# A graph layer's opening reordered: searches, flags, splits and the first block's chunk sums placed behind the first product

## The chip, the cores and the metric

The kernel runs on one core of a Trainium2 chip, in one launch. The metric is the device time of the whole launch in microseconds, smaller is better. The five engines with a queue of their own are TensorE (PE in the profile, with PEld for its weight loads), VectorE (DVE), ScalarE (ACT), GpSimd (POOL) and SyncE (SP, which here only issues DMAs). Each executes its queue in the order in which the program emits it.

## The reference

```python
def ref(x, src, dst, edge_attr, W1, b1, W2, b2):     # x 6250x64, 206250 edges sorted by dst
    h = max(layernorm(x), 0)
    msg = h[src] + edge_attr                          # edge_attr 206250x64
    agg = segment_sum(msg, dst, 6250)
    return x + relu(agg @ W1 + b1) @ W2 + b2          # W1 64x128, W2 128x64
```

All is float32. The edges come sorted by destination node; each node has some 33 of them.

## The kernel before, in words

The sum over `h[src]` is done as a product with counts: for each target node and each of the 6250 source nodes, how many edges go from one to the other. A source node's number is split into a low digit (128 rows) and a high one (49 values). For a *tile* of up to 127 edges of three neighbouring target nodes (a *triple*), TensorE multiplies a one-hot of the low digit by a one-hot of the high digit weighted by the node within the triple (`count`, line 957, out `pc`, 12 tiles at a time); ScalarE copies the counts out of PSUM into a ring in SBUF (line 966). For a *block* of 84 tiles (252 target nodes) TensorE then multiplies the table `h`, split into an upper and a lower half so that the product is exact enough (`h2`, written by `split_upper` and `split_lower`), by the counts: `products` (line 976), 49 matmuls into `pv`, in four parts of 12 or 13. VectorE makes the codes (`encode`, 927 and 933) and the one-hots (`rows_of_tiles`, 944, `hotb`).

The sum over `edge_attr` goes another way: *chunks* of 42 nodes' edges are loaded in order (`load_chunk`, 462, `feat`), VectorE makes a one-hot of each edge's distance to its chunk's first node (`chunk_hot`, 475, `hotf`), and TensorE sums (`chunk_sum`, 486, into `bank`, 48 matmuls). `take_sums` (494) copies a block's sums out, and `chunk_place` (516) adds them to the block's product. `open_gathers` lets GpSimd copy one element of those sums, so that its later gathers stand behind it. The distances come from a gather (`fetch_dst`) at indices that `chunk_columns` and `chunk_index` make; `chunk_nodes` subtracts (426, 427), `chunk_turn` transposes (434, 435) into `rel`.

The last 20 groups of edges are done by gathering rows of a table of `h` in DRAM (`fetch_h`, `hrows`), which `norm_h` writes in three thirds after scaling (595, 596).

To know where a group of tiles begins in the sorted list, the kernel fetches rows of 256 destinations (`fetch_row`), searches in them on ScalarE (`seek`, 354, with a read-back of the accumulator), and writes the starts (`place`, 359 and 361). With them it fetches the edges' packed words in pairs (`fetch_pair`), unpacks them on VectorE in four pieces (`unpack`: fields, offsets, inside, digits), transposes them (`turn_keys` 763, `turn_values` 770) and copies the keys and powers to `kq` and `kv` (783, 791). Fourteen triples with more than 127 edges get a second tile each: `second_ends`, `second_flags`, `second_ranks`, `second_picks`, `second_words`, `second_found` find them, alternating between VectorE and TensorE (`pnext`, `prk`, `pxn`), and `second_fetch` and one more `unpack` bring them in.

The order of all this is written out by hand. The main loop runs over 318 *steps* of six tiles, 14 to a block; block 0's counts are steps 0 to 13, and block `b`'s product runs in steps 1, 3, 5 and 7 of block `b+1` (block 0's in steps 15, 17, 19, 21). The table `before` says what is emitted ahead of a step's count, `SPLITS`, `CLEARS` and `SECOND` add to it, `turn_later` and `at_step` put work behind a step. GpSimd's gathers stand in a list `queue`, drawn from by a planned clock (`pool_until`), except where a function issues them at once.

```python
    for n in range(NSTEP):
        b, s = block_of(n)
        for f in tops.get(n, []) + before.get(n, []):
            f()
        if n % 2:
            count(n)
        if n % (HT // ST) == 0:
            rows_of_tiles(n // (HT // ST) + 1)
        if n % (EB // ST) == AHEAD and n // (EB // ST) * EB + EB < TILES:
            encode(n // (EB // ST) + 1)
        if b and 1 <= s < FRESH:
            products(b - 1, PART[s], PART[s + 1])
        ...
        for f in later.pop(n, []) + turns.pop(n, []):
            f()
```

Of the kernel before, what the change touches and what calls it, by code (L numbers as in the profile page):

```python
# [22 lines left out]
P = 128  # L23
# [41 lines left out]
NX = 14  # L65
# [14 lines left out]
SPLITS = (9, 10, 11)  # L80
CLEARS = (61, 47, 33, 19, 17)
SECOND = (10, 11, 12, 13, 14, 15, 16)
# [3 lines left out]
FIRST_CHUNKS = ((13, 13), (14, 14), (14, 14))  # L86
FIRST_HOT_AT = (11, 12, 14)
# [65 lines left out]
def gnn_kernel(ctx: ExitStack, tc: tile.TileContext, x, src_t, dst_t, dst_g, edge, w1, b1, w2, b2, out):  # L153
# [242 lines left out]
    def chunk_columns(t0, t1, tag="po", bufs=1):  # L396

        px = ps.tile([P, NT + 1], F32, tag=tag, name="pcols", bufs=bufs)
        quarters = known.pop(("q", t0))
        rows = [(t, quarters[:, (t - t0) * RC:(t - t0 + 1) * RC, :]) for t in range(t0, t1)]  # L400
        if t0 == 0:
            rows.append((NT, row_n))
        for t, of in rows:
            nc.tensor.matmul(px[:, t:t + 1], of.rearrange("o c q -> o (c q)"), ones[0:1, 0:1], start=True, stop=True)
        known["t", t0] = px
# [59 lines left out]
    def load(u):  # L465
        for k in range(GB):
            load_chunk(u, k)
# [247 lines left out]
    def unpack(i0, n, p, base, checked):  # L715
        words = words_of.pop(i0)[:p, :n]
        code = late.tile([P, 3, 2, 2, P], I16, name="code")
# [156 lines left out]
    def second_fetch():  # L874
        queue.insert(0, (WORDS_US / 2, lambda: fetch_words(2 * PC, 1, NX, [flags.pop("i")[:, :]])))
# [263 lines left out]
    fetch_pair(2)  # L1139
# [5 lines left out]
    chunk_columns(0, 2, "pc", 2)  # L1145
    seek(7, 4)
# [3 lines left out]
    def first_loads():  # L1150
# [5 lines left out]
        1: [lambda: norm_h(0), lambda: chunk_index(0, 2), lambda: fetch_dst(0), lambda: fetch_dst(1)],  # L1156
        2: [lambda: norm_h(1), lambda: norm_h(2), lambda: [fetch_h(g) for g in range(GA, GA + ROWS)]],
        3: [first_loads, lambda: seek(11, 2)],
        4: [lambda: load(1)],
        5: [lambda: seek(13, IC - 13), lambda: load(2)],  # L1160
        6: [lambda: place(7, IC - 7)],
        8: [lambda: chunk_nodes(0)],
        9: [lambda: chunk_turn(0)],
        16: [find_groups],
# [43 lines left out]
    for i in range(1, IC):  # L1208
        c0, c1 = columns(i)[0][2], columns(i)[-1][2] + columns(i)[-1][1] - columns(i)[-1][0]
        n = min((n for n in range(deadline(c0) + 1 - TURN[-1][0]) if n % STEPS in (TURNS if i > 2 else (2,)) and c1 - R <= encoded(n)),  # L1210
# [8 lines left out]
    n = 23  # L1219
    assert n + TURN[-1][0] <= deadline(SX)  # L1220
    unpack_later(n - 4, lambda: unpack(2 * PC, 1, NX, second_b, NX))
    turn_later(n, 2 * PC, NX, [(0, NX, SX)])
    for t in range(1, NT):
        n = 78 + 14 * t
        before.setdefault(n, []).append(lambda t=t: t > 1 and queue.insert(0, (GATHER_US, lambda: fetch_dst(t))))
        n = 33 if t == 1 else 87 + 14 * t
# [23 lines left out]
    for b in range(NW):  # L1250
# [6 lines left out]
        if b < NW - 1:  # L1257
            at_step(n + STEPS + TAKE, take_sums, b)
            at_step(n + STEPS + TAKE, open_gathers, b)
            for u in of_block[b]:  # L1260
                at_step(n + STEPS + PLACE, chunk_place, u)
# [237 lines left out]
```

## Time and profile before

| | |
|---|---|
| Median of three runs | 400.97 us (399.53 to 402.68) |
| Profiled execution | 401.95 us, its span 399.9 us |
| TensorE busy | 334.5 us (84%) |
| VectorE busy | 321.0 us (80%) |
| ScalarE busy | 322.8 us (81%) |
| GpSimd busy | 240.4 us (60%) |
| DMA | 77.73 MB, mean 194 GB/s |
| Mean granted clock of TensorE | 0.987 |

The span is the time from the first to the last instruction; what lies around it is the launch. A row of the order in time reads: start and length in us, engine, line, operation, what it writes and from what, how many instructions were merged, and in brackets how long the engine stood idle ahead of it and what ended that. A queue's own entries have a q behind the engine's name. A row of the windows has the busy time and the count of instructions of PE, PEld, DVE, ACT and POOL, then the granted clock, the busy share of the DMA engines and GB/s.

### The profile page before, as it was taken

How to read it: one execution, taken by the hardware profiler on the slowest of the kernel's cores; microseconds unless marked ns; L12 is line 12 of the kernel's file. 1: busy time of each engine (PE TensorE's matmuls, PEld its weight loads, DVE VectorE, ACT ScalarE, POOL GpSimd, SP SyncE). 2: the span in 40 equal slices, each digit the busy share in tenths (PEclk: the TensorE clock that was granted, in tenths of full speed). 3: DMA queues.
4: the chain of work that ended last, by engine and by line, in shares of the span. 5: the costliest groups of instructions: out<-in, count | busy, mean ns of one | idle time of the engine just before them, and what ended most of it. 6: DMA issues, size and time to landing. Idle time of an engine off the chain costs nothing.

```text
span 399.9 us, 17302 instructions
## 1 busy us (share of the span) xinstructions
PE 334.5 (84%) x7299; PEld 307.1 (77%) x7300; DVE 321.0 (80%) x833; ACT 322.8 (81%) x376; POOL 240.4 (60%) x254
## 2 busy tenths in 40 slices
PE   2025259689988899989999999999999999999993
PEld 1024149688987798877889988999998999999882
DVE  5969694799899778996789896998799889978620
ACT  5446876669998777898899999999899889988740
POOL 8888687746775665744745677738776576501200
PEclk9999999989998999999999999999999999999998
DMA  7946957556958576684975786786679678755600
GB/s 161 285 126 204 319 140 215 156 147 201 227 180 253 131 221 166 178 264 127 275 219 154 237 247 185 221 259 201 203 236 261 178 200 262 200 161 183 174 11 10
DMA packets 97345, 77.73 MB, mean 194 GB/s; under 512 B 14388, under 2 KB 90284, under 8 KB 97262
## 3 DMA queue, kind: packets, MB, share of 16 engines
q1 hardware_dynamic: 88480, 66.72, 54.9%
q0 software_dynamic: 6544, 9.06, 9.8%
q8 instruction: 59, 0.97, 1.0%
q10 hardware_dynamic: 2238, 0.79, 0.8%
q14 instruction: 24, 0.20, 0.1%
HBM read 72.29 MB, written 4.26 MB: 191 GB/s over the span
## 4 chain that ended last, share of the span: by engine, by line
PE 52%; DVE 15%; ACT 10%; issue 3%; DVEq 0%; ACTq 0%
PE pv L976 26%; PE pc L957 8%; ACT ring L966 7%; PE bank L486 6%; DVE hotb L944 5%; PE po L1062 3%; PE pv L516 2%; PE ph L1054 2%; PE bank L547 2%; DVE hotf L475 2%; PE pk L763 1%; ACT over L892 1%; ACT after L1056 1%; DVE sums L1011 1%; DVE at L927 1%
## 5 line engine op out<-in xcount | busy, mean ns | idle before, releaser
L966 ACT ACTIVATE ring<-pc 128x1764 fp32r<-128x1764 uint8 (+3 forms) x181 | 258.2, 1478 | 23.6 <-PE pc L957 19.4
L336 POOL DMA_INDIRECT hrows<-table,src_p x156 | 174.9, 1121 | 46.1 <-issue 42.3
L976 PE MATMUL pv<-ring,h 128*128 128x252 f32 (+1 forms) x1127 | 154.7, 287 | 0.8 <-ACT ring L966 0.8
L976 PEld LDWEIGHTS pv<-ring,h 128*128 128x128 f32 x1127 | 138.4, 190 | 1.0 <-ACT ring L966 0.9
L944 DVE TENSOR_TENSOR hotb<-at,of 127x576 int32<-127x576 bf16 x212 | 118.5, 600 | 1.0
L957 PE MATMUL pc<-hotb 128*128 128x49 fp8e5 x1904 | 78.1, 187 | 8.9 <-DVE hotb L944 5.6
L957 PEld LDWEIGHTS <-hotb 128*128 128x128 fp8e5 x1904 | 68.2, 99 | 18.7 <-DVE hotb L944 6.0
L486 PE MATMUL bank<-feat,hotf 128*18 128x64 f32 x3240 | 62.2, 227 | 0.9 <-DVE hotf L475 0.6
L1109 POOL COPY root<-after 1x1 f32<-1x1 f32 x22 | 12.5, 569 | 77.4 <-DVE after L494 76.1
L486 PEld LDWEIGHTS bank<-feat,hotf 128*18 128x18 f32 x3240 | 49.8, 101 | 4.3 <-DVE hotf L475 1.1
L475 DVE TENSOR_TENSOR hotf<-rel,iota 128x432 f32<-128x432 bf16 x68 | 40.7, 599 | 1.0 <-PE bank L486 1.0
L783 ACT ACTIVATE kq<-pk 128x512 bf16<-128x512 f32 (+17 forms) x48 | 17.9, 465 | 9.3 <-PE pk L763 9.3
L1011 DVE TENSOR_TENSOR sums<-sums,pv 128x252 f32<-128x252 f32 (+3 forms) x28 | 8.4, 327 | 20.5 <-PE pv L976 20.5
L927 DVE TENSOR_TENSOR at<-iota_a,kq 128x576 bf16<-128x576 bf16 (+1 forms) x53 | 23.9, 450 | 0.2
L336 POOL DMA_INDIRECT words<-packed,first_i x15 | 20.9, 1394 | 4.4 <-issue 3.7
L1056 ACT ACTIVATE after<-ph,b1s 128x252 f32<-128x252 f32 (+3 forms) x26 | 12.1, 464 | 10.2 <-PE ph L1054 10.1
L336 POOL DMA_INDIRECT sums<-in_dst_g,row_i x15 | 17.5, 1167 | 4.6 <-issue 4.3
L1062 PE MATMUL po<-w2s,after 128*126 128x64 f32 (+3 forms) x104 | 16.4, 280 | 3.4 <-ACT after L1056 3.2
L1054 PE MATMUL ph<-sums,w1s 128*128 128x252 f32 (+3 forms) x52 | 16.9, 406 | 2.2 <-DVE sums L1023 1.3
L933 DVE TENSOR_TENSOR of<-of,kv 128x288 bf16<-128x288 bf16 (+1 forms) x53 | 16.4, 310 | 2.3
L1062 PEld LDWEIGHTS po<-w2s,after 128*126 128x126 f32 (+3 forms) x104 | 13.5, 188 | 6.2 <-ACT after L1056 4.9
L763 PE MATMUL pk<-identb,code 128*128 128x128 bf16 (+1 forms) x64 | 10.8, 326 | 7.9 <-DVE code L744 7.9
(189 smaller groups left out, 323.8 us busy)
## 6 DMA issues: line engine op xcount, KB each, us to landing
feat<-in_edge SPq DMA_DIRECT2D x135, 384.0 KB
pfeat<-in_edge SPq DMA_DIRECT2D x19, 256.0 KB
hrows<-table,src_p POOLq DMA_INDIRECT x156
out_y<-after SPq DMA_DIRECT2D x23, 63.0 KB
xl<-in_x SPq DMA_DIRECT2D x2, 512.0 KB
table<-xl SPq DMA_DIRECT2D x2, 512.0 KB
after<-in_x SPq DMA_DIRECT2D x4, 252.0 KB
table<-xl SPq DMA_DIRECT2D x1, 544.0 KB
```

The source lines that it names most:

```text
L336: nc.gpsimd.indirect_dma_start(out=rows, out_offset=None, in_=source, in_offset=bass.IndirectOffsetOnAxis(ap=index, axis=0), compute_op=op)
L475: nc.vector.tensor_tensor(hot_of[u][:, :n].rearrange("p c j w -> p (c j) w"), rel[:, c:c + n].rearrange("p c q k -> p (c q k)").unsqueeze( ...
L486: nc.tensor.matmul(bank[q * QP:q * QP + WQ, at:at + D], hot_of[u][:, c, j, :], feats[u][c][:, j, :], start=(k == 0), stop=(k == JP - 1))
L783: nc.scalar.activation(kq[:, q, at:at + n].rearrange("s i k o -> s (i k) o"), pk[:, q, a:a + n].rearrange("s i k -> s (i k)").unsqueeze(2) ...
L927: nc.vector.tensor_tensor(to[:, :n].rearrange("s i k (m o) -> s (i k) m o", o=2), iota_k.rearrange("s (m o) -> s m o", o=2).unsqueeze(1).t ...
L933: nc.vector.tensor_tensor(pairs_of, pairs_of, kv[:, c:c + n].rearrange("s i k o -> s (i k) o").unsqueeze(2) .to_broadcast([P, 2 * n, WE // ...
L944: nc.vector.tensor_tensor(hot[:SLOTS, :n, c:c + m * A8].rearrange("s i (w a) -> s i w a", a=A8), at[:SLOTS, o:o + n, k].unsqueeze(2).to_br ...
L957: nc.tensor.matmul(pc[:, j * WPC:j * WPC + HI], hot[:, :P], hot[:, P:P + HI], start=True, stop=True)
L966: nc.scalar.activation(to[:, h0:h1], of[:, h0:h1, u:v, :V], AF.Copy)
L976: nc.tensor.matmul(pvs[b], h2[:, h, :], ring[:, h, c:c + columns_of_block(b)], start=(h == 0), stop=(h == HI - 1))
L1054: nc.tensor.matmul(ph[:, :n], w1s, agg[:, start[b]:start[b + 1]], start=True, stop=True)
L1062: nc.tensor.matmul(po[:pairs[b], k, :], hid[:, k:2 * pairs[b]:2], w2s, start=True, stop=True)
```

## The change

No arithmetic is added or removed, with one buffer's exception; the order is changed, in the first 70 steps.

- `fetch_pair(2)` and `seek(7, ...)` leave the part ahead of the loop. The searches 7 to 14 come in pairs at steps 10, 12, 14, 16 (before: four ahead of the loop, then steps 3 and 5), `place` of them at 18 (before: 6).
- Step 1 keeps `norm_h(0)`; the columns, the index and the two distance fetches come at step 2, and only then the pair fetch; `norm_h(1)` and `norm_h(2)` come at step 3 behind the address arithmetic and the first feature loads (before: step 2). `chunk_columns` is cut in two, the constant column (`chunk_numbers`) staying ahead of the loop.
- `chunk_nodes(0)` and `chunk_turn(0)` come at steps 5 and 6 (before: 8 and 9); those of chunk row 1 at 48 and 50 (before: 33 and 35).
- The splits of `h` come at 8, 12 and 15 (before: 9, 10, 11), each `split_lower` one step later.
- Block 0's chunk sums run at 13, 15 and 16 (before: 13, 14, 14), its one-hots at 9, 11 and 14, `take_sums` and `open_gathers` at 17 (before: 14), `chunk_place` at 20 (before: 17).
- The six functions of the triples run at 19 to 24 (before: 10 to 15), `second_fetch` at 24 issues at once (before: from the list, at 16), their `unpack` starts at 33 (before: 19), their turn at 37 (before: 23). Their codes get a buffer of their own, in the tile `after`.
- The turn of keys for tiles 128 to 255 moves from step 2 to 6, `find_groups` from 16 to 13, the first two residual loads from 40 and 44 to 50 and 54, their bias additions with them.

```diff
@@ -77,14 +77,16 @@
 TURN = ((0, "k"), (1, "0"), (2, "1"), (2, "v"), (3, "p"))
 
 
-SPLITS = (9, 10, 11)
+SPLITS = (8, 12, 15)
 CLEARS = (61, 47, 33, 19, 17)
-SECOND = (10, 11, 12, 13, 14, 15, 16)
+SECOND = (19, 20, 21, 22, 23, 24, 24)
 PART = (0, 0, 12, 12, 24, 24, 36, 36, HI)
 CHUNKS = ((9, 9), (11, 11), (13, 13))
 FEATS = 6
-FIRST_CHUNKS = ((13, 13), (14, 14), (14, 14))
-FIRST_HOT_AT = (11, 12, 14)
+FIRST_CHUNKS = ((13, 13), (15, 15), (16, 16))
+FIRST_HOT_AT = (9, 11, 14)
+FIRST_TAKE = 3
+FIRST_PLACE = 6
 LAST_CHUNKS = ((4, 4), (8, 8))
 HOT_AT = (3, 6, 10)
 LAST_HOT_AT = (2, 5)
@@ -393,16 +395,20 @@
                                 row_e.unsqueeze(1).to_broadcast([1, n, JQ]), op=OP.add)
         known["q", t0] = quarters
 
-    def chunk_columns(t0, t1, tag="po", bufs=1):
-
-        px = ps.tile([P, NT + 1], F32, tag=tag, name="pcols", bufs=bufs)
+    def chunk_column(px, t, of):
+        nc.tensor.matmul(px[:, t:t + 1], of.rearrange("o c q -> o (c q)"), ones[0:1, 0:1], start=True, stop=True)
+
+    def chunk_columns(t0, t1):
+
+        if ("t", t0) not in known:
+            known["t", t0] = ps.tile([P, NT + 1], F32, tag="po", name="pcols", bufs=1)
         quarters = known.pop(("q", t0))
-        rows = [(t, quarters[:, (t - t0) * RC:(t - t0 + 1) * RC, :]) for t in range(t0, t1)]
-        if t0 == 0:
-            rows.append((NT, row_n))
-        for t, of in rows:
-            nc.tensor.matmul(px[:, t:t + 1], of.rearrange("o c q -> o (c q)"), ones[0:1, 0:1], start=True, stop=True)
-        known["t", t0] = px
+        for t in range(t0, t1):
+            chunk_column(known["t", t0], t, quarters[:, (t - t0) * RC:(t - t0 + 1) * RC, :])
+
+    def chunk_numbers():
+        known["t", 0] = ps.tile([P, NT + 1], F32, tag="po", name="pcols", bufs=1)
+        chunk_column(known["t", 0], NT, row_n)
 
     def chunk_index(t0, t1):
         px = known.pop(("t", t0))
@@ -712,9 +718,9 @@
 
     unpacked = {}
 
-    def unpack(i0, n, p, base, checked):
+    def unpack(i0, n, p, base, checked, code=None):
         words = words_of.pop(i0)[:p, :n]
-        code = late.tile([P, 3, 2, 2, P], I16, name="code")
+        code = late.tile([P, 3, 2, 2, P], I16, name="code") if code is None else code
         both = code[:p, 0, :, :n]
         low = words.bitcast(I16).rearrange("p i (s o) -> p i s o", o=2)[..., 0]
         node = late.tile([P, 2, P], I32, name="node")[:p, :n]
@@ -872,7 +878,8 @@
         flags["i"] = second_i
 
     def second_fetch():
-        queue.insert(0, (WORDS_US / 2, lambda: fetch_words(2 * PC, 1, NX, [flags.pop("i")[:, :]])))
+        pool[0] += WORDS_US / 2
+        fetch_words(2 * PC, 1, NX, [flags.pop("i")[:, :]])
 
     RP = 4
     bad = small.tile([P, 2 + 2 * RP], F32, name="bad")
@@ -1136,14 +1143,12 @@
     everything = packed.rearrange("(q k) o -> q (k o)", k=P * J)
     nc.sync.dma_start(everything[Q1:], dstn[:, 1])
     nc.sync.dma_start(everything[:Q1], dstn[:Q1, 0])
-    fetch_pair(2)
     chunk_starts(0, 2 * RC, "pc", 2)
     encode(0)
     rows_of_tiles(0)
     chunk_rows(0, 2 * RC)
     chunk_quarters(0, 2)
-    chunk_columns(0, 2, "pc", 2)
-    seek(7, 4)
+    chunk_numbers()
     pools[0].__exit__(None, None, None)
     ring = ctx.enter_context(pools[1]).tile([P, HI, (STEPS + FRESH) * SC], F32R, name="ring")
 
@@ -1153,15 +1158,19 @@
         load(0)
 
     before = {
-        1: [lambda: norm_h(0), lambda: chunk_index(0, 2), lambda: fetch_dst(0), lambda: fetch_dst(1)],
-        2: [lambda: norm_h(1), lambda: norm_h(2), lambda: [fetch_h(g) for g in range(GA, GA + ROWS)]],
-        3: [first_loads, lambda: seek(11, 2)],
+        1: [lambda: norm_h(0)],
+        2: [lambda: chunk_columns(0, 2), lambda: chunk_index(0, 2), lambda: fetch_dst(0), lambda: fetch_dst(1),
+            lambda: fetch_pair(2), lambda: [fetch_h(g) for g in range(GA, GA + ROWS)]],
+        3: [first_loads, lambda: norm_h(1), lambda: norm_h(2)],
         4: [lambda: load(1)],
-        5: [lambda: seek(13, IC - 13), lambda: load(2)],
-        6: [lambda: place(7, IC - 7)],
-        8: [lambda: chunk_nodes(0)],
-        9: [lambda: chunk_turn(0)],
-        16: [find_groups],
+        5: [lambda: load(2), lambda: chunk_nodes(0)],
+        6: [lambda: chunk_turn(0)],
+        10: [lambda: seek(7, 2)],
+        12: [lambda: seek(9, 2)],
+        14: [lambda: seek(11, 2)],
+        16: [lambda: seek(13, IC - 13)],
+        18: [lambda: place(7, IC - 7)],
+        13: [find_groups],
         87: [lambda: chunk_starts(2 * RC, NC)],
         89: [lambda: chunk_rows(2 * RC, NC)],
         90: [lambda: chunk_quarters(2, NT)],
@@ -1207,7 +1216,7 @@
 
     for i in range(1, IC):
         c0, c1 = columns(i)[0][2], columns(i)[-1][2] + columns(i)[-1][1] - columns(i)[-1][0]
-        n = min((n for n in range(deadline(c0) + 1 - TURN[-1][0]) if n % STEPS in (TURNS if i > 2 else (2,)) and c1 - R <= encoded(n)),
+        n = min((n for n in range(deadline(c0) + 1 - TURN[-1][0]) if n % STEPS in (TURNS if i > 2 else (6,) if i < 2 else (2,)) and c1 - R <= encoded(n)),
                 key=lambda n: (i > 2 and TURNS.index(n % STEPS), -n))
         if i > 1 and i % 2 == 0:
             k = 9 if i > 2 else 4
@@ -1216,14 +1225,15 @@
             unpack_later(n - k, lambda i=i: unpack_pair(i))
         assert n <= (NW - 1) * STEPS + 7
         turn_later(n, i, P, columns(i))
-    n = 23
+    n = 37
     assert n + TURN[-1][0] <= deadline(SX)
-    unpack_later(n - 4, lambda: unpack(2 * PC, 1, NX, second_b, NX))
+    unpack_later(n - 4, lambda: unpack(2 * PC, 1, NX, second_b, NX, after[:, :3 * 2 * 2 * P // 2].bitcast(I16)
+                                       .rearrange("p (a b c s) -> p a b c s", a=3, b=2, c=2)))
     turn_later(n, 2 * PC, NX, [(0, NX, SX)])
     for t in range(1, NT):
         n = 78 + 14 * t
         before.setdefault(n, []).append(lambda t=t: t > 1 and queue.insert(0, (GATHER_US, lambda: fetch_dst(t))))
-        n = 33 if t == 1 else 87 + 14 * t
+        n = 48 if t == 1 else 87 + 14 * t
         before.setdefault(n, []).append(lambda t=t: chunk_nodes(t))
         before.setdefault(n + 2 + (t > 1), []).append(lambda t=t: chunk_turn(t))
 
@@ -1232,7 +1242,7 @@
         return n * HEAD_US if n < STEPS else STEPS * HEAD_US + (n - STEPS) * STEP_US
 
     for g in range(len(kept)):
-        n = 40 + 4 * g if g < 2 else 94 if kept[g][2] == 2 else XB * g * STEPS + 10
+        n = 50 + 4 * g if g < 2 else 94 if kept[g][2] == 2 else XB * g * STEPS + 10
         before.setdefault(n, []).append(lambda g=g: residual(g))
         before.setdefault(min(n + 12, NSTEP - 1), []).append(lambda g=g: add_b2(g))
 
@@ -1255,10 +1265,10 @@
             for c in range(units[u][2]):
                 at_step(n + at_c[c], chunk_sum, u, c)
         if b < NW - 1:
-            at_step(n + STEPS + TAKE, take_sums, b)
-            at_step(n + STEPS + TAKE, open_gathers, b)
+            at_step(n + STEPS + (TAKE if b else FIRST_TAKE), take_sums, b)
+            at_step(n + STEPS + (TAKE if b else FIRST_TAKE), open_gathers, b)
             for u in of_block[b]:
-                at_step(n + STEPS + PLACE, chunk_place, u)
+                at_step(n + STEPS + (PLACE if b else FIRST_PLACE), chunk_place, u)
 
     h_next = added = GA
 
```

## The prediction

> **What bounds the kernel now.** I read the stages first: busy time of each engine in ten-microsecond windows (then granted clock and DMA share).
>
> ```profile
> 60.00:70.00 10.00, 10.00 (x200) 9.45 (x195) 4.71 (x14) 6.35 (x5) 7.71 (x5) 1.00 0.73 214
> ...
> 100.00:110.00 10.00, 9.93 (x259) 9.06 (x259) 8.19 (x20) 9.74 (x10) 7.87 (x8) 1.00 0.92 226
> ...
> 250.00:300.00 50.00, 49.60 (x1092) 46.23 (x1095) 44.73 (x118) 47.29 (x56) 35.24 (x35) 1.00 0.74 224
> ```
>
> From 100 us on TensorE is 97 to 99% busy: a microsecond won before that stage moves everything behind it by as much, and one won elsewhere must come off TensorE's queue. So the change is decided before 100 us, and there I read the four queues in order of time (start, length, instruction, wait ahead and its releaser). TensorE:
>
> ```profile
> 52.91 0.58 PE L823 MATMUL pnext<-ends,shift 128*128 128x15 f32 x2 [3.14 <-DVE ends L821]
> ...
> 58.73 0.93 PE L861 MATMUL pxn<-fl,pick 128*14 128x2 f32 x30 [1.67 <-DVE pick L852]
> ...
> 60.28 2.72 PE L486 MATMUL bank<-feat,hotf 128*18 128x64 f32 x93
> ...
> 63.44 2.46 PE L976 MATMUL pv<-ring,h 128*128 128x252 f32 x12
> ...
> 66.06 1.62 PE L976 MATMUL pv<-ring,h 128*128 128x252 f32 x12
> 67.61 0.55 PE L516 MATMUL pv<-select,after 128*64 128x42 f32 x12
> ...
> 69.98 0.67 PE L547 MATMUL bank<-after,pfeat 128*64 128x42 f32 x16
> ...
> 72.89 0.87 PE L486 MATMUL bank<-feat,hotf 128*18 128x64 f32 x48
> 76.11 0.37 PE L763 MATMUL pk<-identb,code 14*128 14x14 bf16 x4 [2.36 <-DVE code L744]
> ...
> 79.27 1.49 PE L486 MATMUL bank<-feat,hotf 128*18 128x64 f32 x48 [0.18 <-DVE hotf L475]
> ...
> 81.20 2.15 PE L976 MATMUL pv<-ring,h 128*128 128x252 f32 x12
> 84.58 0.70 PE L763 MATMUL pk<-identb,code 128*128 128x128 bf16 x4 [1.24 <-DVE code L744]
> ```
>
> The first product (pv) starts at 63.44. Ahead of it stand chunk sums (bank) and the flags' matmuls (pnext, prk, pxn); from 58.73 to 73.76 TensorE has no gap at all, so putting the product ahead of the others only changes the order of that stretch. It then stands 2.36 us for the triples' digits, and falls to half rate: 48 chunk matmuls take 0.87 us at 72.89 and 1.49 at 79.27. At 60.28 they ran at half rate too (93 in 2.72, 29 ns each against 18), though the windows print a granted clock of 1.00 there: up to 63 us matmul durations are the better witness.
>
> ```profile
> 31.91 0.52 ACT L354 ACTIVATE sums<-sums,nhalf 128x256 bf16<-128x256 int32 x1
> ...
> 33.18 0.51 ACT L354 ACTIVATE sums<-sums,nhalf 128x256 bf16<-128x256 int32 x1
> ...
> 37.61 1.64 ACT L966 ACTIVATE ring<-pc 128x1764 fp32r<-128x1764 uint8 x1 [3.19 <-DMA sums<-in_dst_g,row_i]
> 39.15 0.66 ACT L783 ACTIVATE kq<-pk 128x496 bf16<-128x496 f32 x2
> ...
> 49.31 0.49 ACT L435 ACTIVATE rel<-pdst 128x384 bf16<-128x384 f32 x1 [1.59 <-PE pdst L434]
> 49.81 1.06 ACT L606 ACTIVATE h<-sums 128x1024 fp32r<-128x1024 f32 x1
> ...
> 55.49 3.21 ACT L966 ACTIVATE ring<-pc 128x1764 fp32r<-128x1764 uint8 x3
> ```
>
> ScalarE fills the ring. Its first copy waits until 37.61 for the last row fetch and gives way 1.54 later; two steps' copies at 55.49 took 3.21. A key copy costs 0.53 (two overlap in 0.66), a split 1.0, and two searches with their read-backs 1.27 (31.91 to 33.18). It waits for the distances' transposes until 49.31 and ends step 13's copy at 58.70.
>
> ```profile
> 37.04 0.14 DVE L409 CAST cols_i<-pcols 128x2 int32<-128x2 f32 x1
> ...
> 37.24 2.41 DVE L595 SCALAR_TENSOR_TENSOR xl<-xl,sums 128x1024 f32<-128x1024 f32 x2
> ...
> 41.41 1.12 DVE L944 TENSOR_TENSOR hotb<-at,of 127x576 int32<-127x576 bf16 x2
> 44.69 0.17 DVE L359 SCALAR_TENSOR_TENSOR first<-first,middle 128x8 f32<-128x8 f32 x1 [2.17 <-ACT sums L354]
> ...
> 47.17 0.42 DVE L426 TENSOR_SCALAR dstq<-dstq,cols 128x384 f32<-128x384 int32 x1 [1.07 <-DMA dstq<-in_dst_g,cols_i]
> 47.62 0.62 DVE L427 SCALAR_TENSOR_TENSOR dstq<-iota_q,cols,dstq 128x384 f32<-128x384 int16 x1
> ...
> 63.09 0.56 DVE L494 COPY after<-bank 128x384 f32<-128x384 f32 x1 [3.05 <-PE bank L486]
> ...
> 65.72 0.59 DVE L475 TENSOR_TENSOR hotf<-rel,iota 128x432 f32<-128x432 bf16 x1
> ...
> 71.86 0.21 DVE L726 TENSOR_SCALAR code<-words 14x128 int16<-14x128 int16 x1 [4.09 <-DMA words<-packed,second_i]
> ...
> 77.58 1.12 DVE L944 TENSOR_TENSOR hotb<-at,of 127x576 int32<-127x576 bf16 x2
> ...
> 84.24 0.29 DVE L744 TENSOR_SCALAR code<-code 128x512 int16<-128x512 int16 x1
> ```
>
> VectorE waits 2.17 us for searches (the `place` at 44.69), 1.07 for distances, 3.05 for chunk sums and 4.09 for the triples' words. That last wait is the stall TensorE shows at 76.11.
>
> **The change, part by part.** The sum is made against the profiled execution, 401.95 us (span 399.9 and 2.05 around it), which is 0.98 above the median 400.97; I subtract the same gain from the median.
>
> ```profile
> 35.03 2.91 POOL L336 DMA_INDIRECT words<-packed,first_i  x1 [0.30 <-DVE quarters L392]
> 38.24 2.82 POOL L336 DMA_INDIRECT words<-packed,first_i  x1 [0.31 <-issue]
> 41.37 0.95 POOL L336 DMA_INDIRECT dstq<-in_dst_g,cols_i  x1 [0.30 <-DVE src_p L694]
> ...
> 45.27 1.28 POOL L336 DMA_INDIRECT hrows<-table,src_p  x1 [1.70 <-DVE first L359]
> ```
>
> *Distance fetches ahead of `norm_h(1)`, `norm_h(2)` and the pair fetch.* The two word fetches at 35.03 and 38.24 lasted 2.91 and 2.82 instead of 0.95, beside the scaling of x (STT rows, 37.24). The index is written at 37.04 in both kernels, and GpSimd is now free, so the fetch issues at 37.3 instead of 41.37. It had ended its issue at 42.32 and landed by 47.17, 4.85 later; with that, it lands at 43.2. VectorE's own queue arrives there at 37.4 + two scalings 2.4 + encode and table rows 1.8 (from their end at 39.65 to 41.41) + one-hots 1.05 (two overlapping in 1.12) = 42.6, so it waits 0.6. Landing bounds: 41 (as a free queue would, then VectorE's 42.6 decides) and 46.3 (3 us behind table and feature writes). The pair fetch, now behind, is wanted at step 26 only.
>
> The Trainium skill, "GPSIMD Engine Reference", section "1. Specifications", says GpSimd's SBUF interfaces contend with VectorE instructions that have two SBUF inputs; by that rule the encode beside the fetch would stretch it too, as it did the word fetches, by 1.9 us. The trace speaks against it for this shape: the fetch at 41.37 took 0.95 beside the hotb row at 41.41, which has two SBUF inputs.
>
> *Searches (`seek` 7 to 14) behind.* `place` leaves step 6, so VectorE's 2.17 us wait goes; searches 7 to 10 had lain in ScalarE's 3.19 us wait and cost nothing there. Now three of the four pairs stand ahead of step 15's copy, two of them ahead of step 13's: 2.54 us added to a queue that has no cover. Late next is the ring: distances subtracted by 44.1, transposes and copy 1.57 (48.24 to 49.81) to 45.7, then keys 1.58, copies of steps 7, 9, 11, 13 at 1.55, two splits 2.0, searches 2.54: **58.0** for the first product, 5.4 earlier than 63.44. The other moves ahead of that (splits at 8, 12, 15; keys at 6) are inside this count; VectorE reaches the last split at 57.3, before its product at step 19.
>
> ```profile
> 37.14 2.86 SPq L596 DMA_DIRECT2D table<-xl  x3
> ```
>
> *SyncE and the row fetches.* Two feature loads now go between the table's writes, which wait for scalings until 41.6 instead of 39.6. The row fetches waited for the table until 45.27, 5.3 behind its last issue; now about 46.5, first eight landed by 59. `add_rows` at step 16 waits for that at most until 59.6; VectorE waits until 63.5 there anyway, for the last chunk sum. Cover: 4 us.
>
> *TensorE from 58.0.* The order is now product, two chunk sums, then the rest: product at half rate 3.2 (twice 1.6), chunk sum 1.4, chunk sum at full rate 0.85, count and product of step 17 1.9 (0.32 and 1.6 from 66.06 on); ends 65.4. Here the change adds a wait: `second_ends` stands on VectorE behind `take_sums` 0.55, two one-hots of features 0.95 (0.59 the one at 65.72, overlapping), `place` 0.3 (44.69; itself behind the last searches, 63.1) and hotb 1.05, so its result comes at 66.5 and TensorE, with count(19) and its product queued behind pnext, stands 1.1. Then pnext 0.6, count and product 1.95, group sum 0.6, placing 0.5, prk 0.45 (15 matmuls at the 31 ns of pxn's 30 in 0.93), count and product 1.9, pxn 1.5 (58.73 to 60.28), count 0.4: count(23) ends at **74.4**, against 72.9 before. The early start is spent: the sums and flags merely moved into it. Bounds of this part: the clock up by the start of the sums and no stall, 72.3; half rate lasting 6.1 us as it did from 58.73 to 64.8 (five of the twelve matmuls at 63.44 slow), 75.2.
>
> The clock's page ("TensorE: Matmul & The Clock Gate", section "Part 1: The HAM clock gate", the Trainium skill) gives about 3.4 us of sustained work before full rate, which from 58.0 would be 61.4 and 0.5 us better than my count; the 6.1 us between 58.73 and 64.8 here disagree, the 3 from 79.27 to the fourth matmul or so of the group at 81.20 agree.
>
> *Triples apart (own `code`, unpacked from step 33, words fetched at 24 without a queue place).* The 4.09 us wait goes, since nine steps lie between fetch and use, where three did. What is late next is ScalarE: copies 23, 25, 27 from 74.4, 4.65, so block 1's product starts at 79.1 instead of 81.20, and at full rate. VectorE has its answer from pxn at 74.2 and then the work that stood between 77.58 and 84.7 (hotb to second digit row; 7.1): the pair's keys come at 81.4 instead of 84.58. **Gain 3.2 us.**
>
> *What arrives later.* VectorE gets the triples' unpacking, twelve instructions of 0.21 (71.86), 2.5 us, in steps 33 to 36 and loses `chunk_nodes(1)`, 0.95 (as 47.17 to 48.16): +1.55. Its one-hots lead the counts there by a trio of steps, about 1.5 us; if that lead were gone already, all of it would show. `chunk_turn(1)`, 0.5 on ScalarE (49.31) and about as much on TensorE, goes from step 35 to 50, into the window 100 to 110, where both are full (9.93 and 9.74 of 10): 0.5 lost. The bias additions go from steps 52 and 56 to 62 and 66, one stretch in which VectorE feeds the count at 67 as before: 0, or their 1.2 us (2 at 0.6 as one-hots of like size) if that count then waits. Groups and residuals: DMA issues and small rows beside full queues, 0 (0.3 without cover).
>
> Sum: 3.2 - 0.5 = 2.7. Profiled 401.95 - 2.7 = 399.25; median **398.3**.
>
> **Rivals.**
> ```profile
> 124.00:126.00 2.00, 2.00 (x46) 1.81 (x37) 1.93 (x6) 1.09 (x2) 0.00 (x0) 0.50 1.08 331
> ```
>
> 1. *The handovers cost nothing.* TensorE's 1.1 us stall shrinks and full rate comes with the first sum (2.0 better, the bound 72.3); with VectorE earlier by as much, keys at 79.4 and a gain of 4.7; the half-rate spell that the last row shows, well behind, may go too: some 2 us at 0.50, so about 1 more. For: VectorE is idle 4 us in the same stretch. Against: its queue is in order. 395.3 to 396.3.
>
> 2. *The distances land late.* All of ScalarE's copies hang on them with nothing between; 1.9 us as the word fetches were stretched gives a gain of 0.8, 400.2. For: two feature loads and a table write now issue just with the fetch, and among feature loads it took 4.85 before. Against: it was four loads then. GpSimd's rule above, of the Trainium skill, would give this time.
> 3. *Slower: the clock falls in the handovers.* If the gaps at pnext and prk drop TensorE to half rate as the 2.36 us gap did, the products of steps 19 and 21, pxn's neighbours and the sum of 23 take about 1.6 + 1.6 + 0.4 + 0.6 = 4.2 more: count(23) at 78.5, 1.5 slower in all, 402.5. It decides as soon as the gaps exceed 2 us together within one spell; I count 1.1.
> 4. *The change moves no bound:* if VectorE's 1.55 and one search pair more, 1.27, both land on the path, the gain is -0.1 and the time 401.1.
>
> **How the numbers follow.** Chances: forecast (gain 2 to 4) 0.43, rival 1 0.35, rivals 2 and 4 together 0.13, rival 3 0.09. One per cent, 4 us, is about what a measurement tells here (three runs span 399.53 to 402.68). Rival 1 is mostly beyond it, with a little of the forecast's edge: faster 0.38. Rival 3 needs a late landing besides to exceed it: slower 0.06. The rest, 0.56, is within. The range reaches from rival 1's better end, less the 1.4 by which the lowest run lies under its median, to rival 4 with its remainder: 394.0 to 401.5.
>
> **What would show it.** First product at 57 to 59; distances read by 43.2; TensorE waiting for pnext near 65 by about 1; no wait for words of `second_i`; block 1's product near 79 at full rate; pair's keys at 81.4. Wrong if copies stand long after 46, if TensorE rests over 2 us between 58 and 74, or if a stretch behind 100 us that was full shows new waits.

## The result, and the profile after

The changed kernel takes 403.55 us (median of 16 runs, 401.05 to 405.38), the kernel before 401.14 (16 runs, 399.11 to 402.68): a ratio of 1.0056, 95% interval 1.0034 to 1.0078. It is **slower by half a per cent**; the forecast was 398.3 and a range up to 401.5. The profiled execution took 403.83, its span is 402.1 (399.9 before). Ratios and intervals, here and below, leave out every run more than 1.5% above the fastest of its kernel.

TensorE's queue after the change, in order of time. Line numbers have shifted: the product is now L983, the chunk sums L492, the keys' transposes L769.

```profile
57.19 2.93 PE L983 MATMUL pv<-ring,h 128*128 128x252 f32 x12 [1.83 <-ACT ring L973]
60.05 2.31 PE L492 MATMUL bank<-feat,hotf 128*18 128x64 f32 x96
...
62.60 1.65 PE L983 MATMUL pv<-ring,h 128*128 128x252 f32 x12
71.22 0.61 PE L829 MATMUL pnext<-ends,shift 128*128 128x15 f32 x2 [6.97 <-DVE ends L827]
...
72.58 2.91 PE L983 MATMUL pv<-ring,h 128*128 128x252 f32 x12
...
77.05 1.74 PE L983 MATMUL pv<-ring,h 128*128 128x252 f32 x13
...
84.94 1.65 PE L983 MATMUL pv<-ring,h 128*128 128x252 f32 x12
87.60 0.70 PE L769 MATMUL pk<-identb,code 128*128 128x128 bf16 x4 [1.02 <-DVE code L750]
```

The first product starts at 57.19 instead of 63.44, earlier than forecast (58.0), and the part for step 17 starts at 62.60. Then TensorE stands for 6.97 us, where 1.1 was forecast, and works at half rate when it comes back: twelve matmuls of the product at 72.58 take 2.91 us, and 1.65 at 62.60 and 84.94. Block 1's product starts at 84.94, 3.7 later than before, the pair's keys at 87.60, 3.0 later. Some 0.8 of these is not the change's: VectorE writes the index of the distance fetches at 37.86 here and at 37.04 in the profile before, but the changed kernel's variants below, alike up to there, write it anywhere from 36.95 (e1) to 38.19 (e9). What TensorE waits for is `second_ends` on VectorE:

```profile
43.26 0.41 DVE L432 TENSOR_SCALAR dstq<-dstq,cols 128x384 f32<-128x384 int32 x1
...
56.47 1.28 DVE L617 TENSOR_TENSOR h<-xl,sums 128x1088 fp32r<-128x1088 f32 x1
67.66 0.69 DVE L1123 TENSOR_TENSOR pfeat<-pfeat,hrows 128x512 f32<-128x512 f32 x1 [9.90 <-issue]
68.28 0.55 DVE L500 COPY after<-bank 128x384 f32<-128x384 f32 x1
...
69.95 1.12 DVE L951 TENSOR_TENSOR hotb<-at,of 127x576 int32<-127x576 bf16 x2
71.00 0.17 DVE L827 TENSOR_SCALAR ends<-first 128x15 f32<-128x15 f32 x1
```

VectorE ends the last split at 57.75 and then waits 9.90 us ahead of the sum of the first fetched rows of h (L1123, `add_rows`). The last column says "issue" because the profile names no releaser there; the operands are `pfeat`, loaded long before, and `hrows`. Behind that sum stand `take_sums` (68.28), one-hots (69.95) and `second_ends` (71.00), and behind `second_ends` the rest of TensorE's queue. GpSimd's queue has the fetches of those rows:

```profile
50.84 1.72 POOL L338 DMA_INDIRECT hrows<-table,src_p  x1 [6.35 <-DVE sums L611]
...
62.62 0.94 POOL L338 DMA_INDIRECT hrows<-table,src_p  x1 [0.30 <-issue]
```

They start at 50.84, after a wait of 6.35, and the eighth ends its issue at 63.56. In the kernel before they started at 45.27, and the sum found them there without a wait:

```profile
65.12 0.67 DVE L1116 TENSOR_TENSOR pfeat<-pfeat,hrows 128x512 f32<-128x512 f32 x1
```

They read the table, which SyncE writes:

```profile
37.96 0.33 SPq L602 DMA_DIRECT2D table<-xl  x1
39.84 0.98 SPq L468 DMA_DIRECT2D feat<-in_edge  x2
41.13 1.55 SPq L602 DMA_DIRECT2D table<-xl  x2
```

Two feature loads (39.84) stand ahead of the table's last two writes (41.13 to 42.68). The table is read 8.2 us after the last issue; before, with no feature load ahead, it was 5.3 after (40.00 to 45.27).

All other waits that the change was to remove did go: the triples' words are no longer waited for, `place` no longer waits for searches while block 0 is counted, and the distances are read at 43.26 without a wait.

How the loss runs through the kernel is seen from the last part of each block's product, which I took from TensorE's queue in order of time:

| start of the last part, us | block 0 | block 1 | block 2 | block 6 | block 21 |
|---|---|---|---|---|---|
| before | 70.90 | 90.73 | 103.91 | 164.93 | 381.34 |
| after | 77.05 | 93.41 | 107.05 | 167.00 | 383.61 |

It is 6.2 late in block 0, recovers half by block 1, because the triples' stall has gone, and stays between 1 and 4 from there to the end, 2.3 at block 21. So the stages behind 100 us carried the difference through, as forecast, only with the other sign.

### The profile page after: what moved, and what is told of

The parts are those of the page before. It is cut to its first block, busy times and chain, and to the rows that moved or that the text cites. A ratio compares the mean times of both kernels' runs of the same rounds, so it can differ in the third digit from the quotient of the medians.

```text
span 402.1 us, 17279 instructions
## 1 busy us (share of the span) xinstructions
PE 334.5 (83%) x7299; PEld 307.1 (76%) x7300; DVE 321.1 (80%) x833; ACT 322.1 (80%) x376; POOL 229.0 (57%) x254
## 4 chain that ended last, share of the span: by engine, by line
PE 53%; DVE 26%; ACT 8%; issue 7%; DMA 2%; POOL 1%; DVEq 1%; ACTq 0%
PE pv L983 26%; PE pc L964 8%; DVE hotb L951 7%; PE bank L492 6%; ACT ring L973 5%; PE po L1069 3%; PE ph L1061 2%; DVE hotf L481 2%; PE pv L522 2%; PE bank L553 2%; POOL hrows L338 1%; PE pk L769 1%; DVE at L934 1%; ACT over L899 1%; DMA words<-packed,first_i 1%
## 5 line engine op out<-in xcount | busy, mean ns | idle before, releaser
L338 POOL DMA_INDIRECT hrows<-table,src_p x156 | 171.5, 1099 | 50.9 <-issue 43.6
L983 PE MATMUL pv<-ring,h 128*128 128x252 f32 (+1 forms) x1127 | 156.0, 289 | 2.6 <-ACT ring L973 2.6
L983 PEld LDWEIGHTS pv<-ring,h 128*128 128x128 f32 x1127 | 139.4, 192 | 3.1 <-ACT ring L973 2.9
L492 PE MATMUL bank<-feat,hotf 128*18 128x64 f32 x3240 | 60.8, 225 | 1.9 <-DVE hotf L481 1.3
L492 PEld LDWEIGHTS bank<-feat,hotf 128*18 128x18 f32 x3240 | 48.7, 100 | 5.4 <-DVE hotf L481 1.7
L1116 POOL COPY root<-after 1x1 f32<-1x1 f32 x22 | 5.8, 262 | 80.7 <-DVE after L500 80.6
L1123 DVE TENSOR_TENSOR pfeat<-pfeat,hrows 128x512 f32<-128x512 f32 (+1 forms) x20 | 13.5, 674 | 10.6 <-issue 9.9
L338 POOL DMA_INDIRECT words<-packed,first_i x15 | 18.0, 1202 | 4.4 <-issue 4.3
```

Of the source, the lines that this page charges most:

```text
L338: nc.gpsimd.indirect_dma_start(out=rows, out_offset=None, in_=source, in_offset=bass.IndirectOffsetOnAxis(ap=index, axis=0), compute_op=op)
L492: nc.tensor.matmul(bank[q * QP:q * QP + WQ, at:at + D], hot_of[u][:, c, j, :], feats[u][c][:, j, :], start=(k == 0), stop=(k == JP - 1))
L983: nc.tensor.matmul(pvs[b], h2[:, h, :], ring[:, h, c:c + columns_of_block(b)], start=(h == 0), stop=(h == HI - 1))
```

## Experiments

The theory T: the time is lost in VectorE's wait ahead of `add_rows`; the rows are late because the table is late, and the table because two feature loads precede its writes on SyncE's queue. The rivals: U, the handovers between VectorE and TensorE and the half clock cost the time wherever the wait stands; T2, the fetches themselves are slow, whatever the table does. All ratios are to the kernel before, of runs on the same chip; chips differ from one experiment to another. Since the opening shifts by up to 1.2 us between executions, e5 also gives times counted from the index of the distance fetches, which stands ahead of the edits of all these experiments.

### e1: the sum of rows held back

```diff
-            if added in parts_of and fetched.get(added, 1e9) + LAND_US <= clock(n):
+            if added in parts_of and fetched.get(added, 1e9) + LAND_US <= clock(n) and (n >= 23 or added > GA):
```

> The changed kernel with one edit: the first add_rows (the sum of the first eight fetched rows of h) is held until step 23 instead of standing at step 16. Theory T (the time is lost in VectorE's 9.90 us wait ahead of that sum, behind which take_sums, place, one-hots and second_ends stand): the wait goes, take_sums runs right behind the last chunk sum, near 62.5 us instead of 68.28, TensorE's 6.97 us wait for pnext shrinks to 1 or 2, block 1's product comes at 79 to 80 instead of 84.94, and the median falls by 4 to 5.5, to 398 to 399.5. Rival U (the handovers between VectorE and TensorE in steps 17 to 24 and the half clock cost the time, the sum of rows only stands where another wait would): the wait moves to the next instruction, 402.5 to 403.5.

Measured: the twelve runs scatter from 394.58 to 406.00, with a median of 400.94; the ratio of 0.9937 (0.9893 to 0.9982) is that of the lowest five, up to 400.16. Their median, 399.52, is at the upper edge of T's forecast; the median of all twelve is 2.6 below the changed kernel's 403.55 and no lower than the kernel before (401.02). So the time settles little, and the profile (of a run of 399.76) has to. VectorE's queue and one row of TensorE's:

```profile
61.93 0.56 DVE L500 COPY after<-bank 128x384 f32<-128x384 f32 x1 [5.09 <-PE bank L492]
...
78.56 0.69 DVE L1123 TENSOR_TENSOR pfeat<-pfeat,hrows 128x512 f32<-128x512 f32 x1 [3.76 <-DMA hrows<-table,src_p]
```

```profile
64.48 0.40 PE L829 MATMUL pnext<-ends,shift 128*128 128x15 f32 x2 [0.88 <-DVE ends L827]
...
75.50 1.65 PE L983 MATMUL pv<-ring,h 128*128 128x252 f32 x12
82.30 1.04 PE L769 MATMUL pk<-identb,code 128*128 128x128 bf16 x4 [5.15 <-DVE code L750]
```

The wait is gone from the first sum: `take_sums` runs at 61.93, TensorE stands 0.88 ahead of pnext, and block 1's product starts at 75.50. U falls: with the wait away, the same handovers let the product come 9.4 us earlier (8.5 counted from the index). But the second sum of rows now waits 3.76 for its own fetches (78.56, here the profile names them), ahead of the pair's digits, and TensorE stands 5.15 for the keys at 82.30. Holding one sum back hides the late rows once; the second sum, reached sooner than in the changed kernel, waits instead, and the third, at 94.13, does not.

### e2: the scaling and the table's writes ahead of the features

```diff
-        3: [first_loads, lambda: norm_h(1), lambda: norm_h(2)],
+        3: [lambda: norm_h(1), lambda: norm_h(2), first_loads],
```

> The changed kernel with the scaling of the second and third part of x (norm_h) ahead of the address arithmetic and the first feature loads within step 3, so that VectorE scales some 0.9 us earlier and SyncE issues the table's writes ahead of the features. Theory T1 (the rows are late because the table lands late, 50.84, and that because feature loads stand ahead of its writes): the row fetches start at 46 to 47.5, the wait ahead of add_rows falls from 9.9 to 5 or 6, the median falls by 3 to 4, to 399.5 to 400.5. Rival T2 (the rows are late because the fetches themselves are slow beside the splits and the feature loads behind them): start moves by 1 us at most, median 402.5 to 403.5.

Measured: 395.80, ratio 0.9863 (0.9828 to 0.9897). The rows' fetches start at 46.42 and their sum at 62.76, after a wait of 5.87, in the range forecast by T1, though the profile is of the one run of 401.00, where the other six lie between 394.09 and 396.63; the gain against the changed kernel, 7.75, is twice what was expected. T2 falls, for the start moved by 4.4. Nor do the fetches last longer where they come late: the eight take 11.9 us in the kernel before (45.27 to 57.12), 12.7 in the changed one and 13.3 in e3, the next experiment.

### e3: only the feature loads moved

`load(0)` is taken out of `first_loads` and put behind the two `norm_h`; VectorE's order stays that of the changed kernel.

```diff
-        3: [first_loads, lambda: norm_h(1), lambda: norm_h(2)],
+        3: [first_loads, lambda: norm_h(1), lambda: norm_h(2), lambda: load(0)],
```

> The changed kernel with VectorE's order as it is, and only the first two feature loads moved behind the table's writes in SyncE's order. T1 by SyncE's order: the row fetches start at 47 to 48, the median falls by 2.5 to 3.5, to 400 to 401. If VectorE's order (scaling later) were the cause of the late table: start at 50 still, 403 to 403.5.

Measured: 395.91, ratio 0.9890 (0.9851 to 0.9928). SyncE, GpSimd, VectorE and TensorE:

```profile
37.22 4.69 SPq L602 DMA_DIRECT2D table<-xl  x3
43.55 19.91 SPq L468 DMA_DIRECT2D feat<-in_edge  x12
```

```profile
45.86 0.94 POOL L338 DMA_INDIRECT hrows<-table,src_p  x1 [2.11 <-DVE of L934]
...
58.21 0.95 POOL L338 DMA_INDIRECT hrows<-table,src_p  x1 [0.30 <-issue]
```

```profile
60.97 0.69 DVE L1123 TENSOR_TENSOR pfeat<-pfeat,hrows 128x512 f32<-128x512 f32 x1 [3.89 <-issue]
61.60 0.56 DVE L500 COPY after<-bank 128x384 f32<-128x384 f32 x1
```

```profile
56.44 2.92 PE L983 MATMUL pv<-ring,h 128*128 128x252 f32 x12 [1.83 <-ACT ring L973]
...
64.59 0.40 PE L829 MATMUL pnext<-ends,shift 128*128 128x15 f32 x2 [1.39 <-DVE ends L827]
...
65.36 1.65 PE L983 MATMUL pv<-ring,h 128*128 128x252 f32 x12
...
76.12 1.65 PE L983 MATMUL pv<-ring,h 128*128 128x252 f32 x12
79.34 0.70 PE L769 MATMUL pk<-identb,code 128*128 128x128 bf16 x4 [1.58 <-DVE code L750]
```

With the two feature loads moved behind the two table writes and nothing else, the fetches start at 45.86 instead of 50.84, the sum of rows runs at 60.97, 6.7 earlier, and just ahead of the end of the last chunk sum; TensorE's wait falls from 6.97 to 1.39, the product at 65.36 runs at full rate (1.65 against 2.91), and block 1's product starts at 76.12, 8.8 earlier; 0.7 of each of these is the shift of the opening (index at 37.12 against 37.86). The profile is 395.84 against 403.83. SyncE's order is thus shown as the cause, and VectorE's order (scaling 0.9 later) as worth nothing that these runs show: e2, which changes both, has the same median (395.80 and 395.91). Whether the two writes are late because they stand in one queue with the loads, or because the loads occupy the DMA engines, was not separated; loads from another queue were not tried. The size was underestimated, since the half-rate product and the waits behind the late rows went with the wait. The Trainium skill, "DMA: Bandwidth & Descriptors", section "Queues, rings and completion order", says that on each DMA engine descriptors are consumed in ring order; the writes that wait behind loads here agree with that.

### e5: one feature load ahead

```diff
         table_rows(src_p, src_hi)
-        load(0)
+        load_chunk(0, 0)
...
-        3: [first_loads, lambda: norm_h(1), lambda: norm_h(2)],
+        3: [first_loads, lambda: norm_h(1), lambda: norm_h(2), lambda: load_chunk(0, 1)],
```

> The changed kernel with one of the first two feature loads ahead of the table's last two writes in SyncE's order and the other behind them. If each load ahead costs its share (T1, dose and effect): the row fetches start at 47.5 to 49, between 45.86 with none ahead and 50.84 with both, VectorE's wait ahead of add_rows is 6 to 8, the median 398 to 401. If only the order as such counts (any load ahead and the writes lose their turn): start at 50 to 51 and 402.5 to 403.5.

Measured: 398.38, ratio 0.9931 (0.9898 to 0.9964); fetches from 47.46, sum at 63.47 after a wait of 5.78, pnext after one of 2.42. GpSimd and VectorE:

```profile
47.46 1.29 POOL L338 DMA_INDIRECT hrows<-table,src_p  x1 [3.07 <-DVE of L940]
```

```profile
63.47 0.69 DVE L1123 TENSOR_TENSOR pfeat<-pfeat,hrows 128x512 f32<-128x512 f32 x1 [5.78 <-issue]
```

| loads ahead of the last two writes | index written, us | first row fetch, us | between them | ratio |
|---|---|---|---|---|
| none (e3) | 37.12 | 45.86 | 8.7 | 0.9890 |
| none (e7) | 36.99 | 45.66 | 8.7 | |
| none (e2) | 37.05 | 46.42 | 9.4 | 0.9863 |
| one (e5) | 37.77 | 47.46 | 9.7 | 0.9931 |
| two (changed kernel) | 37.86 | 50.84 | 13.0 | 1.0056 |
| two (e1) | 36.95 | 50.61 | 13.7 | |
| two (e9) | 38.19 | 51.49 | 13.3 | |

The ratio is given where the kernels differ in these loads and the scaling alone. Two loads delay the table's reader by 3.6 to 5.0 us, one by 1.0 at most: an effect that grows with the dose, most of it with the second load. In time, two loads stand clear of one; the intervals of none (e3) and one overlap.

### e6: the converse, on the kernel before

```diff
-        2: [lambda: norm_h(1), lambda: norm_h(2), ...
+        2: [lambda: load(0), lambda: norm_h(1), lambda: norm_h(2), ...
```

(The line goes on unchanged; `load(0)` leaves `first_loads`.)

> The converse on the kernel before: the first two feature loads issued ahead of the table's last two writes, nothing else. T1: the row fetches start at 49 to 50.5 instead of 45.27. But the sum of rows stands at 65.12 there without a wait, since the flags and both chunk sums stand ahead of it: rows that land near 65 or 66 cost 0 to 1.5, median 401 to 402.5. If a late table costs as much as it did in the changed kernel whatever stands around it: 405 to 408.

Measured: 401.11, ratio 1.0026 (1.0000 to 1.0053). GpSimd and VectorE:

```profile
51.53 0.98 POOL L336 DMA_INDIRECT hrows<-table,src_p  x1 [8.31 <-DMA table<-xl]
```

```profile
66.40 0.69 DVE L1116 TENSOR_TENSOR pfeat<-pfeat,hrows 128x512 f32<-128x512 f32 x1 [0.80 <-DMA hrows<-table,src_p]
```

The fetches are as late as in the changed kernel (51.53), and yet the sum of rows waits 0.80. The table's lateness costs by what stands ahead of its reader: here VectorE reached that sum at 65.6 (65.12 in the kernel before), in the changed one at 57.75. The reader had moved earlier and the data later, each by several microseconds.

### e4 and e8: the triples alone

On the kernel before, only: `SECOND = (19, 20, 21, 22, 23, 24, 24)`, their fetch at once, their codes in `after`, unpacked from step 33, turned at 37; chunk row 1 at 48 and residuals at 50 and 54 with them.

> The kernel before with only the triples' part of the change: flags at steps 19 to 24, their words fetched at 24, their digits unpacked from step 33 into a buffer of their own, the turn at 37, chunk row 1's distances at 48 and 50, residuals at 50 and 54. By the prediction's term for it (the 4.09 us wait for the triples' words is on the path): TensorE's wait at 76 goes, block 1's product comes 2 to 3 us earlier than 81.20, median 2 to 4 below before, 397 to 399. Rival (the flags in the full stretch and the handovers cost as much as the wait): 400.5 to 401.5.

Measured: ratio 0.9966 (0.9927 to 1.0004). One of the twelve runs took 779.17 and is left out; the others scatter from 396.65 to 402.60, with a median of 400.44, which misses the forecast (397 to 399) and touches the rival's range. The profiled execution, 396.65, is the lowest of them. TensorE:

```profile
61.39 1.75 PE L977 MATMUL pv<-ring,h 128*128 128x252 f32 x12
...
65.63 0.39 PE L823 MATMUL pnext<-ends,shift 128*128 128x15 f32 x2 [0.22 <-DVE ends L821]
...
66.40 1.65 PE L977 MATMUL pv<-ring,h 128*128 128x252 f32 x12
...
76.77 1.67 PE L977 MATMUL pv<-ring,h 128*128 128x252 f32 x12
79.91 0.70 PE L763 MATMUL pk<-identb,code 128*128 128x128 bf16 x4 [1.48 <-DVE code L744]
```

The 2.36 us stall and the half-rate spell behind it are gone, and block 1's product starts at 76.77, 4.4 earlier than in the kernel before; 2 to 3 was expected. That kernel was run again, because its runs scattered:

> The kernel of e4 once more, because its runs lay between 396.65 and 402.6 while its profile showed block 1's product 4.4 us earlier than before. If the gain at block 1 holds and something later takes it back in some runs: a profile of a run near 400 shows block 1's last product part at 85 to 86 as before (90.73 in the kernel before) and a loss behind it, at a half-rate spell. If it is lost at once: block 1's last part at 89 to 91 there.

Measured: 398.80, ratio 0.9958 (0.9922 to 0.9995). Its profile is again of a run near the lower end (397.19), with block 1's last part at 85.85 (85.71 the first time, 90.73 before) and block 21's at 376.71 (376.26; 381.34 before). So in both profiles a gain of 5 us holds from block 1 to the end, measured against a profile of the kernel before that lies 0.9 above its median. Runs near 400 were not caught in a profile: the ratios say that the kernel gains only about 1.5 us. Of the runs of e4 and e8 above 399 us, eight of eleven have a mean granted clock of 0.960 to 0.981; of those below, eight of ten have 0.988 to 0.992. That further half-rate spells take the rest in some executions is therefore likely, and not shown.

### e7: the flags a step later

On the kernel with the features behind: `SECOND = (20, 21, 22, 23, 24, 25, 25)`.

> The kernel of e3 (feature loads behind the table's writes) with the triples' six functions and their fetch one step later, 20 to 25, so that pnext stands behind the count and product of step 19. If TensorE's remaining 1.39 us wait ahead of pnext is on the path: 1 to 1.4 less than e3, 394.3 to 395. If ScalarE's copies or VectorE's queue set the pace there instead: as e3, 395.5 to 396.3, with the wait gone or moved.

Measured: 394.98, ratio 0.9854 (0.9811 to 0.9897), its profile 393.80. TensorE:

```profile
65.95 0.40 PE L829 MATMUL pnext<-ends,shift 128*128 128x15 f32 x2
...
75.44 1.65 PE L983 MATMUL pv<-ring,h 128*128 128x252 f32 x12
78.06 0.70 PE L769 MATMUL pk<-identb,code 128*128 128x128 bf16 x4 [0.98 <-DVE code L750]
```

pnext no longer waits, block 1's product comes 0.7 earlier than with the features behind alone, and the keys 1.3. The medians differ by 0.9, but on two chips on which the kernel before differs by 0.5 as well (401.02 and 400.50), and the intervals of the two ratios overlap, so a gain in time over e3 is not shown; that this version is faster than the changed kernel (403.55) and the kernel before is beyond the noise.

### e9: the reloads held

In the changed kernel the sum started 4.1 us after the eighth fetch's issue; with the features behind it was 1.8. The four feature reloads set off by block 0's second and third chunk sums are held:

```diff
+            if u not in (1, 2):
+                load_chunk(u + FEATS // GB, k)
...
+        20: [lambda: load(4), lambda: load(5)],
```

> The changed kernel with the table's writes behind the feature loads as they are, and only the four feature reloads that block 0's second and third chunk sums set off (at steps 15 and 16) held until step 20. In the changed kernel the eighth row fetch ends its issue at 63.56 and the sum of rows starts at 67.66, 4.1 later, while DMA is at 0.87 to 1.00; with the features behind (e3) that was 59.15 to 60.97, 1.8. If the reloads account for that difference: the sum starts near 65.5, median 401 to 402. If the rows are late by their issue alone: 67 to 68 and 403 to 404.

Measured: 403.21, ratio 1.0046 (1.0018 to 1.0074). A miss in time. VectorE and TensorE:

```profile
66.60 0.69 DVE L1124 TENSOR_TENSOR pfeat<-pfeat,hrows 128x512 f32<-128x512 f32 x1 [8.53 <-issue]
```

```profile
83.60 0.49 PE L492 MATMUL bank<-feat,hotf 128*18 128x64 f32 x18 [1.37 <-issue]
...
85.57 0.53 PE L492 MATMUL bank<-feat,hotf 128*18 128x64 f32 x24 [0.61 <-DMA feat<-in_edge]
```

The eighth fetch's issue ends at 63.87, so the sum follows it by 2.7 instead of 4.1: by these two profiles the reloads account for 1.4. But then the chunk sums of block 1 waited for the held features (1.37 and 0.61), and nothing was won.

## Why the prediction was wrong

**The step that failed** is "SyncE and the row fetches": that the table would be readable at about 46.5, the first eight rows landed by 59, and VectorE's sum covered by 4 us of waiting for the last chunk sum. I named the two loads that pass ahead of the writes, gave them no price, and moved the table by 1.2 us in all (45.27 to 46.5). But they carried 2 x 384 KB into the queue ahead of it: the table came at 50.84, 4.3 later than that. From the table to the last row landed I had 12.5 us, without rows for it, although the eight issues alone take 11.9 in the kernel before; here they took 12.7 (50.84 to 63.56) and the sum came 4.1 behind the last, 16.8 together. So the sum ran at 67.66 where I had its rows by 59. The cover ended at 62.4, with the last chunk sum, so 5.3 us showed, and 1.3 more by the half-rate product behind it. With the loads behind the writes (e3) the sum runs at 60.97 and the cover holds. The sign that I had named for being wrong, TensorE resting over 2 us between 58 and 74, is the 6.97 us ahead of 71.22.

**What the sum had right.** The distances were read at 43.26 (43.2 forecast), but with some luck: I had VectorE ready at 42.6 and waiting 0.6 for them, and it came at 43.26 itself, the opening being 0.8 late, and did not wait. In the profiles the early start of the first product brings little, as the forecast said: e3 starts it 5 us ahead of the kernel with the triples alone (56.44 against 61.39), and block 1's product comes 0.65 earlier. The medians of the same two kernels on one chip say more, 395.91 against 400.44 (ratios 0.9890 and 0.9966): five of e3's six runs lie within 395.54 to 396.37, while those with the triples alone scatter up to 402.60. Why the rest of the change keeps the runs together is open. TensorE's wait ahead of pnext, forecast as 1.1, is 1.39 in e3 and can be removed (e7). Without the failed step the change brings 5.1 by the medians (401.02 to 395.91) and 4.4 by the ratio, where the sum had 2.7.

**Mis-sized terms.** The triples' part was 3.2 in the forecast less 0.5; in the profile of e4 it is 4.4 at block 1's start, and 5 at block 21 in both profiles; by the ratios of e4 and e8 it is 1.4 to 1.7, so that the size of this term differs between the profiled executions and the median. The first product came 1.6 earlier than counted in e3 (56.44 against 58.0). ScalarE's copies ahead of it, in the changed kernel:

```profile
56.63 1.68 ACT L973 ACTIVATE ring<-pc 128x432 fp32r<-128x432 uint8 x2
```

They run to 58.31, and yet the first part of the product starts at 57.19: the copy of step 13 is cut at row 12, and that part, which reads rows 0 to 11, waits for the first piece only. I had counted the whole copy, whose end at 58.31 is near my 58.0.

**The rivals.** None described what happened. The first gives the time of the change without the failed step: it had 395.3 to 396.3 and the pair's keys at 79.4, and e3 has 395.91 and 79.34, also without the half-rate spell at 124 to 126 (granted clock 1.00 there). Its reason is borne out in part only, since the stall ahead of pnext did not shrink. The third had the right sign and a half-rate spell behind a gap in the handovers, with a limit of 2 us for the gap; the gap was 6.97 and the product behind it did fall to half rate, but the gap came from the rows, not from the handovers, which without it cost 1.4. The length of a gap alone does not decide on half rate either: behind 2.24 us ahead of pnext in e2's profile twelve matmuls of the product took 2.91, behind 2.42 in e5's they took 1.65. The second, a landing that comes late behind feature loads, was the right mechanism at the wrong reader: the distances, fetched with the loads, came in time; the rows, fetched from a table written behind the loads, did not.

## What to carry to other kernels

When a step is moved, follow the DMAs that it issues to the reader at the other end: a load that passes a write on the same queue can delay whoever reads what is written (here by about 4 us), and that may be an instruction many steps later on another engine. A cover is a difference of two times, the reader's and the data's; a change that brings the reader forward eats it even when the data stay where they were. And if the work between two points of the busiest engine's queue is full, reordering it moves little (0.65 us between the profiles of e3 and e4); look for the waits that reordering removes, and try them one by one: here two DMA issues in the wrong place took back more than the removed waits gave.

## What was not expected of the hardware

The windows of two microseconds of the changed kernel (PE, PEld, DVE, ACT, POOL busy; granted clock; DMA share; GB/s):

```profile
48.00:50.00 2.00, 0.46 (x12) 0.44 (x12) 2.00 (x5) 2.00 (x5) 0.00 (x0) 1.00 1.02 336
...
66.00:68.00 2.00, 0.00 (x0) 0.00 (x0) 0.34 (x1) 0.73 (x1) 1.39 (x3) 1.00 0.94 309
68.00:70.00 2.00, 0.00 (x0) 0.00 (x0) 1.97 (x7) 0.00 (x0) 1.70 (x2) 0.64 0.21 48
70.00:72.00 2.00, 0.78 (x4) 0.78 (x5) 1.17 (x5) 0.00 (x0) 1.39 (x3) 0.50 0.06 16
```

Two loads of 384 KB ahead of two table writes on the same queue delayed the table's reader by 3.6 to 5.0 us, counted from the index, and one load by 1.0 at most. The DMA engines moved 336 GB/s at 48 to 50, at which one load is 1.2 us and two are 2.3: the second load cost more than its bytes, and why is open. After 6.97 us without a matmul the granted clock is 0.64 and then 0.50 in these windows, and the part of the product at 72.58 runs at half rate; by 77.05 thirteen matmuls take 1.74 again. The gap of 1.39 us in e3 left the next product at full rate.
